# Woven tiles at tiles 11 and 14 of each sixteen, and two explicit orders, in a linear-attention and RWKV feed-forward kernel

## The chip, the cores and the metric

The kernel runs on one core of a Trainium2 chip. A core has a matrix engine (TensorE; PE in the profile, PEld for its weight loads), a vector engine (VectorE; DVE), an activation engine (ScalarE; ACT), GpSimd (POOL) and SyncE (SP), whose queue issues nearly every DMA of this kernel. Each engine takes its own instructions in the order in which the program lists them and waits, where one needs it, on another engine or a DMA. The metric is the device time of one execution in microseconds (us); lower is better.

## The reference, cut to what matters

`x` is (16, 1024, 512) in float32. One post-norm layer is an attention half and a feed-forward half:

```python
qkv = x @ Wqkv.T + bqkv;  q, k, v = split(qkv)
q, k = rope(heads(rmsnorm(q, gq))), rope(heads(rmsnorm(k, gk)))
qf, kf = relu(q), relu(k)
vk  = einsum('bhlp,bhld->bhpd', [v, 1], kf)      # summed over all l of a batch
res = einsum('bhpd,bhld->bhlp', vk, qf)
attn = res[..., :-1] / (res[..., -1:] + EPS_LIN)
x = layernorm(x + rmsnorm(attn @ Wout.T + bout, gout))
# feed-forward: xr, xk mix each row with the row before it
r = sigmoid(xr @ W_r.T);  k = relu(xk @ W_k.T) ** 2
x = layernorm(x + r * (k @ W_v.T))
```

Because `vk` is a sum over a whole batch of 1024 rows, the output of a batch can't begin before all its keys are done.

## The kernel before, in words

The 16 x 1024 rows are cut into 128 tiles of 128 rows, eight to a batch. The program has two stages.

**The key stage** runs over the tiles i = 0 to 127, `early(i)` for the first eight and `slot(i)` for the rest. A plain slot has 36 matmuls of 128x512 on TensorE: 24 for q and k (`proj`, L429), and 12 that add the tile's keys to the batch's sum (`add_kx`, L505, of tile i-1). The projections don't start from zero: a ScalarE copy first puts the bias into the PSUM bank (`seed`, L163; the tiles `psq` and `psk`). On VectorE a slot has the rotary products (`rope`, L461 to L463), the small `ss` (L470), `kl` (L476, the low half of the keys), and the low halves `xl` (L334) and `xnl` (L349) of the next tile's input. q goes out to DRAM (`q_d`, L466).

**Pairs.** When two batches are done, their sums are turned into the combined matrix `m` (value projection, mask, output weights) over the ten slots with i % 16 from 2 to 11: `split_kx` (L588, L589), `finish_pair` (L606, L614, L623 to L635), and `finish_c` (L691 to L695), which multiplies by the output weights with three matmuls into `psm`, splits the result on ScalarE and VectorE into `m`, and stores it. At i % 16 = 1 `finish_a` and `finish_s` empty the sums of a batch out of PSUM and reduce them. `split_kx` and its followers are VectorE's and ScalarE's extra load in these slots.

**Woven tiles.** The output of attention for tile j needs `m` of its batch. For the first eight tiles j = 0 to 7 it is done inside the key stage, woven into its slots, and for j = 8, 9 and 10 a part of it. With FIRST = 30 and STEP = 8 a woven tile j begins at slot i = 30 + 8j: that slot issues the loads of q and x (L209, L225) on SP's queue; the next has `part_q` (L234 to L241: the VectorE instruction `pr`, which is the first to need the loaded q, then a reduction, three small ones, and the scaling of q) and `part_qt` (four transposes on TensorE into `psqt`, L169, then `qth` on ScalarE and `qtl` on VectorE, L252 and L253); the one after has `part_s` (the bias seeded into `psy`), `part_m` (12 matmuls into `psy`, L184) and `part_y` (norm, residual, layer norm: L298 to L306 and L281 to L289). So a woven tile has 16 matmuls of its own on TensorE. The even j begin at i % 16 = 14, the odd ones (38, 54, 70, 86, 102) at i % 16 = 6, in the middle of a pair's ten slots. `load_ks` and `load_m` bring what the woven tiles of a batch read: `ksb` (read by `pr`) and four `mb` (read by `part_m`); both are buffers that batch 1 takes over from batch 0. `late_load` and `late_split` (L720, L722) bring in and split the weights of later stages at slots with i % 16 over 10, through the `xw` buffers, which the loaded x of tiles j >= 4 use too.

Four PSUM banks serve all of `psq`, `psk`, `psqt`, `psy`, `pskv` and `psm` in turn.

**The feed-forward stage** then does the remaining tiles, 128 of feed-forward and 119 of attention output, at some 1450 us.

**What sets the order.** The list of each engine is made at compile time by a planner: it walks the program with estimated durations, and at each point gives an engine the earliest traced instruction that it estimates to be ready. So an instruction that is traced later can be put ahead of one traced earlier. `not_before(ins, last)` (L95) puts an edge into the plan, without a semaphore: `ins` comes after `last` in its engine's list. `in_order` does so for a whole block, and `tc.issue_after(load.ins)` for DMA issues: they come behind the load of `xt` of the same slot.

Of the kernel before, what the change touches and what calls it, by code (L numbers as in the profile page):

```python
# [8 lines left out]
F32 = mybir.dt.float32  # L9
# [6 lines left out]
P = 128  # L16
DIM = 512
# [3 lines left out]
HH = DH // 2  # L21
NPRE = 8
NQ = 3
FIRST, STEP = 30, 8
PAIRS = 7
NWARM = 8
HT = 512
NT = HT // P
# [6 lines left out]
def kernel(  # L35
# [28 lines left out]
    nc = tc.nc  # L64
# [6 lines left out]
    dram = ctx.enter_context(tc.tile_pool(name="dram", bufs=1, space=bass.MemoryType.DRAM))  # L71
# [23 lines left out]
    def not_before(ins, last):  # L95

        tc.add_manual_dep(
            ins,
            last.name,
            mybir.DependencyInfo(mybir.DependencyClass.NoSync, mybir.DependencyReason.DATA),  # L100
            reason="in_order",
        )

    def last_of(engine):
        return next(i for i in reversed(nc.cur_bb.bb.instructions) if i.engine == engine)
# [18 lines left out]
    def bank(name, k=None):  # L124
        if k is not None:
            banks[0] = k
        k = banks[0] % 8
        banks[0] += 1
        if "ps" in own and k >= 4:
            return own["ps"].tile([P, DIM], F32, tag="mm2", bufs=4, name=name)  # L130
        return pp.tile([P, DIM], F32, tag="mm", bufs=4, name=name)
# [69 lines left out]
    def load_ks(b):  # L201
        ksb[b] = ring("ks", b + (b > 0), 1, 1, [P, DIM], F32, f"ksb{b}")
        nc.sync.dma_start(
            out=ksb[b], in_=ks_d[b].rearrange("g p -> (g p)").partition_broadcast(P)
        )

    def load_q(j):
        qs[j] = tp.tile([P, DIM], F32, tag="q", bufs=3, name=f"q{j}")
        nc.sync.dma_start(out=qs[j], in_=q_d[j])  # L209
# [10 lines left out]
    def load_x(j, src=None, early=False):  # L220
        if early and j >= NT:
            xs[j] = tp.tile([P, DIM], F32, tag="xw", bufs=3, name=f"xw{j}")
        else:
            xs[j] = x_tile(j)
        nc.sync.dma_start(out=xs[j], in_=x[j] if src is None else src)  # L225
# [4 lines left out]
    def part_q(j):  # L230

        q = qs[j]
        pr = tp.tile([P, DIM], F32, tag="y", bufs=2, name=f"pr{j}")
        V.scalar_tensor_tensor(pr, q, 0.0, ksb[j // 8], ALU.max, ALU.mult)  # L234
        den = small(HEADS, "den", f"den{j}")
        V.reduce_sum(den, heads(pr), AX.X)
        rs = rstd_all[:, j, 0:1]
        V.tensor_scalar(den, den, rs, EPS_LIN, ALU.mult, ALU.add)
        V.reciprocal(den, den)
        V.tensor_scalar(den, den, rs, None, ALU.mult)  # L240
        V.scalar_tensor_tensor(  # L241
            heads(q), heads(q), 0.0, den.unsqueeze(2).to_broadcast([P, HEADS, DH]), ALU.max, ALU.mult
        )

    def part_qt(j):
        q = qs.pop(j)
        ps = bank(f"psqt{j}")
        transposes(ps, [q[:, c * P : (c + 1) * P] for c in range(NC_)])
        ps = groups(ps)
        th = wp.tile([P, NC_, P], F32R, tag="qth", bufs=2, name=f"qth{j}")  # L250
        tl = wp.tile([P, NC_, P], F32R, tag="qtl", bufs=2, name=f"qtl{j}")
        S.copy(th, ps)  # L252
        V.tensor_sub(tl, ps, f32(th))  # L253
        qT[j] = th, tl
# [3 lines left out]
    def part_s(j):  # L258
        seeds[j] = seeded(f"psy{j}", b_out)

    def part_m(j):
        th, tl = qT.pop(j)
        ps = seeds.pop(j)
        m = [ms[j // 8, c] for c in range(NC_)]
        product(
            ps,
            [((th[:, c, :], tl[:, c, :]), (m[c][:, 0, :], m[c][:, 1, :])) for c in range(NC_)],
            slice(0, P),
            every,
            afresh=False,  # L270
        )
        return ps
# [18 lines left out]
    def part_y(j, ps):  # L291
        for _ in part_y_steps(j, ps):
            pass
# [17 lines left out]
    with ExitStack() as a_ctx:  # L311
# [372 lines left out]
        def finish_c(b, g, place=None):  # L684

            th, tl = fin.pop((b, g))
            if g == 0:
                m_d[b] = dram.tile([P, 2, NC_, DIM], F32, name=f"m_d{b}")
            ps = bank(f"psm{b}{g}", place)
            for n, (a, r) in enumerate(((th, 0), (th, 1), (tl, 0))):  # L690
                T.matmul(ps, lhsT=a, rhs=w_o[g][:, r, :], start=(n == 0), stop=(n == 2))  # L691
            m = te.tile([P, 2, DIM], F32R, tag="m", bufs=2, name=f"m{b}{g}")
            S.copy(m[:, 0, :], ps)
            V.tensor_sub(m[:, 1, :], ps, f32(m[:, 0, :]))
            nc.sync.dma_start(out=m_d[b][:, :, g, :], in_=f32(m))  # L695
# [190 lines left out]
        def late_step(i, load):  # L886
            if staged and staged[0][0] <= i - 2:
                late_split()
            if i == 7:
                with tc.issue_after(load.ins):  # L890
                    constants()
            if i == 12:
                for n in "kr":
                    V.tensor_scalar(omm[n], mu[n], -1.0, 1.0, ALU.mult, ALU.add)

            if late and (3 <= i < 11 or i % 16 > 10 and not 27 <= i < 32):
                with tc.issue_after(load.ins):
                    late_load(i)


        loads_m = {28 + c: (0, c) for c in range(NC_)}
        loads_m.update({n: (1, c) for c, n in enumerate((95, 96, 97, 103))})

        def slot(i):
            last = i == N - 1
            if i + 2 < N:
                load = load_xt(i + 2)
            b, t = divmod(i - 2, 8)
            if b >= 0 and t == 7:
                finish_a(b)  # L910
            qk = [ahead.pop((i, j)) if (i, j) in ahead else proj(i, j) for j in range(2)]
            if not last:
                split_x(i + 1)
            split_xn(i)
            if not last:
                load_xn(i + 1)
            if b >= 0 and t == 7:
                finish_s(b)

            p, u = divmod(i - 18, 16)  # L920
            if 0 <= p < PAIRS and u in (0, 2, 4, 6):
                split_kx(p, u // 2)
            if 0 <= p < PAIRS and u in (1, 3, 5, 7):
                finish_pair(p, u // 2)
            if 0 <= p < PAIRS and 2 <= u < 10:
                finish_c(2 * p + u % 2, u // 2 - 1)
            if i == 8 * 2 * PAIRS + 10:
                finish_b(2 * PAIRS)
            if 0 <= i - 8 * 2 * PAIRS - 11 < NC_:
                finish_c(2 * PAIRS, i - 8 * 2 * PAIRS - 11)  # L930
            add_kx(i - 1)
            for j in range(2):
                rope(i, j, qk[j])
            add_keys(i)
            if not last:
                for j in range(2):
                    rope_table(i + 1, j)
                for j in range(2):
                    seed(i + 1, j)
            if i + 2 < N:  # L940
                late_step(i, load)
            if 0 <= p < PAIRS and u in (0, 1, 3, 4, 5, 7):
                with tc.issue_after(load.ins):
                    if u % 4 == 0:
                        load_ksv(p, u // 4)
                    else:
                        load_wo(u // 2)
            u = i - 8 * 2 * PAIRS - 9
            if 0 <= u < NC_:
                with tc.issue_after(load.ins):  # L950
                    (load_wo, load_wo_last)[u % 2]((0, 2, 1, 3)[u])
            j, late_by = divmod(i - FIRST, STEP)
            if i in loads_m:
                with tc.issue_after(load.ins):
                    load_m(*loads_m[i])
            if j + 1 in (0, NPRE) and late_by == STEP - 1:
                with tc.issue_after(load.ins):
                    load_ks((j + 1) // 8)
            if 0 <= j < NPRE + NQ:
                b = j // 8  # L960
                if late_by == 0:
                    with tc.issue_after(load.ins):
                        load_q(j)
                        load_x(j, early=j < NPRE)
                if late_by == 1:
                    part_q(j)
                    if j <= NPRE:
                        part_qt(j)
                if late_by == 2 and j < NPRE:
                    part_s(j)  # L970
                    part_y(j, part_m(j))
                    if j >= NT:
                        x1_d[j] = dram.tile([P, DIM], F32, name=f"x1_d{j}")
                        nc.sync.dma_start(out=x1_d[j], in_=xs.pop(j))

        x1_d = {}
        tp.tile([P, 56], F32, name="fill_top")
# [299 lines left out]
```

## Time and profile before

| What | us |
|---|---|
| three runs | 2741.31, 2741.24, 2738.0 (median 2741.24) |
| the profiled execution, its own time | 2739.19 |
| its span, first to last instruction | 2737.4 |
| TensorE busy in the span | 2689.9 (98%) |
| VectorE, ScalarE, GpSimd busy | 2197.7, 1909.8, 696.0 |
| mean granted TensorE clock | 0.997 |

The span is from the first to the last instruction that the profiler saw. An engine's busy time leaves out its waits; TensorE's busy time is a union of matmuls whose ends are modelled and overlap, so a stretch that is all busy need not be at full rate. A stretch is best read by three numbers together: its length, the number of matmuls in it, and the clock granted.

In the span the key stage takes about the first 1225 us and the feed-forward stage the rest. In what follows "tile 37 begins at 337.0" means the start of the first `psq` matmul of that tile (L429) in the trace.

### The profile page before, as it was taken

The page shows a single profiled execution, that of the slowest core. Times are in us where ns is not written, and L with a number is a line of the kernel's source. Part 1 is how long each engine was busy: PE and PEld are TensorE (multiplying, and loading weights), DVE is VectorE, ACT ScalarE, POOL GpSimd, SP SyncE. Part 2 cuts the span into 40 slices and gives each one's busy share as a digit, 9 for nine tenths or more (in the row PEclk, how much of TensorE's full clock was granted, in tenths as well). Part 3 has the DMA queues.
Part 4 walks back from the last instruction along what each step waited for, and adds up shares of the span by engine and source line. Part 5 has one row for each costly group of instructions (what it writes and reads, how often), then busy time and mean ns, then how long its engine had stood idle before and what let it go on. Part 6 is the DMA issues. An engine that isn't in the chain of part 4 may idle for free.

```text
span 2737.4 us, 39858 instructions
## 1 busy us (share of the span) xinstructions
PE 2689.9 (98%) x12336; PEld 2214.0 (81%) x12336; DVE 2197.7 (80%) x4852; ACT 1909.8 (70%) x3876; POOL 696.0 (25%) x800
## 2 busy tenths in 40 slices
PE   9999999999999999999999999999999999999998
PEld 7888877777787878887888888888888888888887
DVE  8787777878787887876888888888887888888874
ACT  6666666656666666656778777777777777777775
POOL 5222212222221222224322222222222222222221
PEclk9999999999999999999999999999999999999999
DMA  7888777877777887874323231323223232313210
GB/s 258 291 291 285 235 244 261 270 246 246 234 229 241 265 283 242 277 270 155 108 73 97 94 115 58 113 88 104 74 93 112 63 107 89 119 56 106 79 52 37
DMA packets 241005, 455.80 MB, mean 167 GB/s; under 512 B 25476, under 2 KB 29316, under 8 KB 240792
## 3 DMA queue, kind: packets, MB, share of 16 engines
q1 hardware_dynamic: 240500, 452.73, 51.0%
q8 instruction: 97, 1.59, 0.2%
q14 instruction: 116, 0.95, 0.1%
q10 hardware_dynamic: 292, 0.53, 0.1%
HBM read 334.64 MB, written 118.52 MB: 166 GB/s over the span
## 4 chain that ended last, share of the span: by engine, by line
PE 61%; DVE 3%; DMA 1%; ACT 1%; issue 1%; POOL 0%; POOLq 0%; SPq 0%; DVEq 0%; ACTq 0%
PE psr L184 13%; PE psk L184 12%; PE psv L184 12%; PE psy L184 12%; PE psk L429 3%; PE pskx L505 3%; PE psq L429 3%; PE pst L169 2%; PE psqt L169 2%; PE psm L691 1%; DMA xn<-in_x_dram 0%; DVE t L461 0%; DMA xt<-in_xt_dram 0%; DVE ro L463 0%; DMA q<-q_d 0%
## 5 line engine op out<-in xcount | busy, mean ns | idle before, releaser
L184 PE MATMUL psk<-mkh,w_k 128*128 128x512 f32 x1024 | 332.7, 396 | 1.0 <-DVE kx L531 0.7
L184 PE MATMUL psv<-w_v,kah 128*128 128x512 f32 x1024 | 321.6, 395 | 0.5 <-DVE qtl L253 0.3
L184 PE MATMUL psy<-mb,qth 128*128 128x512 f32 x1024 | 320.2, 390 | 0.4 <-ACT qth L252 0.2
L184 PE MATMUL psr<-w_r,mrh 128*128 128x512 f32 x1024 | 318.6, 396 | 0.0
L184 PEld LDWEIGHTS psy<-mb,qth 128*128 128x128 f32 x1024 | 191.9, 188 | 41.0 <-ACT psy L163 0.8
L487 POOL TENSOR_TENSOR acc<-acc,ro 128x512 f32<-128x512 f32 x96 | 152.7, 1591 | 282.5 <-ACT ro L475 183.3
L184 PEld LDWEIGHTS psk<-mkh,w_k 128*128 128x128 f32 x1024 | 191.2, 188 | 40.1 <-DVE kx L531 0.9
L148 POOL TENSOR_TENSOR rstd_all<-ss,mhalf 128x2 f32<-128x2 f32 x128 | 91.7, 716 | 501.6 <-DVE ss L470 391.5
L184 PEld LDWEIGHTS psr<-w_r,mrh 128*128 128x128 f32 x1024 | 188.7, 188 | 36.8 <-ACT r L1065 0.2
L184 PEld LDWEIGHTS psv<-w_v,kah 128*128 128x128 f32 x1024 | 187.6, 188 | 37.8 <-DVE gate L1155 0.7
L429 PE MATMUL psq<-wqk_h,xh 128*128 128x512 f32 x512 | 202.7, 396 | 15.4 <-ACT psq L163 14.5
L1030 POOL TENSOR_TENSOR mkl<-mixk,mkh 128x512 fp32r<-128x512 f32 x127 | 165.8, 1306 | 181.7 <-ACT mkh L1028 181.7
L429 PE MATMUL psk<-wqk_h,xh 128*128 128x512 f32 x512 | 200.7, 393 | 3.8 <-ACT psk L163 3.8
L429 PE MATMUL psq<-wqk_h,xl 128*128 128x512 f32 x512 | 200.2, 392 | 0.0
L184 PE MATMUL psv<-w_v,kal 128*128 128x512 f32 x512 | 200.1, 391 | 0.0
L429 PE MATMUL psk<-wqk_l,xh 128*128 128x512 f32 x512 | 200.1, 392 | 0.0
L184 PE MATMUL psk<-mkl,w_k 128*128 128x512 f32 x512 | 199.8, 391 | 0.2 <-DVE mkl L1030 0.2
L429 PE MATMUL psq<-wqk_l,xh 128*128 128x512 f32 x512 | 200.0, 392 | 0.0
L429 PE MATMUL psk<-wqk_h,xl 128*128 128x512 f32 x512 | 199.9, 391 | 0.0
L184 PE MATMUL psy<-mb,qtl 128*128 128x512 f32 x512 | 199.6, 390 | 0.0
L184 PE MATMUL psr<-w_r,mrl 128*128 128x512 f32 x512 | 196.5, 393 | 0.0
L474 ACT ACTIVATE kh<-ro,rstd_all 128x512 fp32r<-128x512 f32 x128 | 92.9, 726 | 115.3 <-DVE ro L463 96.5
(208 smaller groups left out, 7119.0 us busy)
## 6 DMA issues: line engine op xcount, KB each, us to landing
tab<-tab_d SPq DMA_DIRECT2D x480, 256.0 KB, 4.5
xt<-in_xt_dram SPq DMA_DIRECT2D x128, 256.0 KB, 4.3
xn<-in_x_dram SPq DMA_DIRECT2D x128, 256.0 KB, 4.5
q_d<-ro SPq DMA_DIRECT2D x128, 256.0 KB, 4.2
m_d<-m SPq DMA_DIRECT2D x64, 512.0 KB, 5.4
mb<-m_d SPq DMA_DIRECT2D x64, 512.0 KB, 6.4
q<-q_d SPq DMA_DIRECT2D x128, 256.0 KB, 2.6
out_dram<-x SPq DMA_DIRECT2D x128, 256.0 KB, 2.0
```

The costliest lines, as they stand in the source:

```text
L148: G.tensor_tensor(dst, src, mhalf[:, 0 : src.shape[1]], ALU.pow)
L169: T.matmul(ps[:, n * P : (n + 1) * P], lhsT=b, rhs=ident, is_transpose=True, start=(n == 0), stop=(n == NC_ - 1), skip_group_check=True,)
L184: T.matmul(ps, lhsT=a[u][:, rows], rhs=b[w][:, cols], start=(afresh and c == 0 and k == 0), stop=(c == n - 1 and k == 2), skip_group_check ...
L429: T.matmul(ps, lhsT=a[i][:, c, :], rhs=w_qk[b][:, c, cols], start=(not seeds and n == 0), stop=(seeds and n == 3 * NC_ - 1), skip_group_ch ...
L474: S.activation(kh, r, AF.Relu, scale=rstd_all[:, i, 1:2])
L487: G.tensor_add(acc[b], acc[b], ros[i])
L505: T.matmul(ps_kx[b][c], lhsT=a[:, c * P : (c + 1) * P], rhs=r, start=(t == 0 and n == 0), stop=(t == 7 and n == 2),)
L691: T.matmul(ps, lhsT=a, rhs=w_o[g][:, r, :], start=(n == 0), stop=(n == 2))
L1030: (V if by_v else G).tensor_sub(ml, m, f32(mh))
```

## The change

A list `WOVEN` takes the place of FIRST and STEP: woven tile j begins at slot `WOVEN[j]`. The even j keep their slots (30, 46, 62, 78, 94, 110); the odd ones move five slots later, from 38, 54, 70, 86, 102 to 43, 59, 75, 91, 107, which is i % 16 = 11. With them move the loads of q and x, `part_q`, `part_qt`, `part_s`, `part_m`, `part_y` and, for j = 5 and 7, the store of x. `late_load` leaves out the slots in `WOVEN`: before, its loads after slot 15 were at 43, 44, 45, 46, 47, 59 and 60; now at 44, 45, 47, 60, 61, 63 and 76. Two of the loads of `m` of batch 1 go from slots 97 and 103 to 108 and 109. `load_ks` of batch 1 stays at slot 93.

Two explicit orders are added. In the woven tiles, the first VectorE instruction of `part_q` (`pr`) comes, in VectorE's list, after the VectorE instruction traced last before it; that is `kl` of its slot, or the last instruction of a `late_split`. In `finish_c`, the first output-weight product comes, in TensorE's list, after the TensorE instruction traced last before it: the end of `proj`, or of `finish_pair` in the slots that have one.

```diff
-FIRST, STEP = 30, 8
+
+WOVEN = (30, 43, 46, 59, 62, 75, 78, 91, 94, 107, 110)
...
+    def behind(engine):
+
+        return last_of(engine), len(nc.cur_bb.bb.instructions)
+
+    def follow(engine, mark):
+        before, n = mark
+        not_before(next(i for i in nc.cur_bb.bb.instructions[n:] if i.engine == engine), before)
...
             ps = bank(f"psm{b}{g}", place)
+            mark = behind(mybir.EngineType.PE)
             for n, (a, r) in enumerate(((th, 0), (th, 1), (tl, 0))):
                 T.matmul(ps, lhsT=a, rhs=w_o[g][:, r, :], start=(n == 0), stop=(n == 2))
+            follow(mybir.EngineType.PE, mark)
...
-            if late and (3 <= i < 11 or i % 16 > 10 and not 27 <= i < 32):
+            if late and (3 <= i < 11 or i % 16 > 10 and not 27 <= i < 32 and i not in WOVEN):
...
-        loads_m.update({n: (1, c) for c, n in enumerate((95, 96, 97, 103))})
+        loads_m.update({n: (1, c) for c, n in enumerate((95, 96, 108, 109))})
...
-            j, late_by = divmod(i - FIRST, STEP)
...
-            if j + 1 in (0, NPRE) and late_by == STEP - 1:
+            for j in (0, NPRE):
+                if i == WOVEN[j] - 1:
+                    with tc.issue_after(load.ins):
+                        load_ks(j // 8)
+            if i in WOVEN:
+                j = WOVEN.index(i)
                 with tc.issue_after(load.ins):
-                    load_ks((j + 1) // 8)
-            if 0 <= j < NPRE + NQ:
-                b = j // 8
-                if late_by == 0:
-                    with tc.issue_after(load.ins):
-                        load_q(j)
-                        load_x(j, early=j < NPRE)
-                if late_by == 1:
-                    part_q(j)
-                    if j <= NPRE:
-                        part_qt(j)
-                if late_by == 2 and j < NPRE:
-                    part_s(j)
-                    part_y(j, part_m(j))
...
+                    load_q(j)
+                    load_x(j, early=j < NPRE)
+            if i - 1 in WOVEN:
+                j = WOVEN.index(i - 1)
+                mark = behind(mybir.EngineType.DVE)
+                part_q(j)
+                follow(mybir.EngineType.DVE, mark)
+                if j <= NPRE:
+                    part_qt(j)
+            if i - 2 in WOVEN[:NPRE]:
+                j = WOVEN.index(i - 2)
+                part_s(j)
+                part_y(j, part_m(j))
...
```

More of the change, by code (lines that the diff above doesn't have):

```diff
@@ L955, in slot @@
                     load_m(*loads_m[i])
-            if j + 1 in (0, NPRE) and late_by == STEP - 1:
-                with tc.issue_after(load.ins):
-                    load_ks((j + 1) // 8)
-            if 0 <= j < NPRE + NQ:
-                b = j // 8
-                if late_by == 0:
-                    with tc.issue_after(load.ins):
-                        load_q(j)
-                        load_x(j, early=j < NPRE)
-                if late_by == 1:
-                    part_q(j)
-                    if j <= NPRE:
-                        part_qt(j)
-                if late_by == 2 and j < NPRE:
-                    part_s(j)
-                    part_y(j, part_m(j))
-                    if j >= NT:
-                        x1_d[j] = dram.tile([P, DIM], F32, name=f"x1_d{j}")
-                        nc.sync.dma_start(out=x1_d[j], in_=xs.pop(j))
+            for j in (0, NPRE):
[4 more added lines that the diff above has]
+                j = WOVEN.index(i)
+                with tc.issue_after(load.ins):
+                    load_q(j)
[11 more added lines that the diff above has]
+                part_y(j, part_m(j))
+                if j >= NT:
+                    x1_d[j] = dram.tile([P, DIM], F32, name=f"x1_d{j}")
+                    nc.sync.dma_start(out=x1_d[j], in_=xs.pop(j))
         x1_d = {}
```

## The prediction

> **What bounds the kernel now.** I read the engine totals first, then stretches of the span, then the one VectorE instruction that the change pins. TensorE is busy 2689.9 of 2737.4 us, so all that can be won is in the 47.5 us in which it idles and in what those gaps cost beside it. The feed-forward stage has none: from 1350 to 2700 us every 50 us are 50.00 us busy. The losses are in the key stage, so I cut it by tiles. First seven tiles each, i % 16 from 5 to 11, the middle of a pair to its end: tiles 21 to 27, which have no woven tile, then 37, 53, 69, 85 and 101, where an odd woven tile runs.
>
> ```profile
> core 0: us, PE busy (x) PEld busy (x) DVE busy (x) ACT busy (x) POOL busy (x), PEclk, DMA share, GB/s
> 191.10:256.80 65.70, 65.70 (x296) 54.53 (x295) 55.26 (x95) 43.35 (x91) 14.48 (x13) 1.00 0.84 271
> 337.00:416.40 79.40, 74.06 (x317) 59.87 (x316) 62.81 (x116) 48.79 (x103) 15.76 (x16) 0.96 0.76 246
> 498.80:576.00 77.20, 71.97 (x313) 58.24 (x312) 61.77 (x111) 48.58 (x103) 15.15 (x15) 0.98 0.77 245
> 658.30:733.80 75.50, 70.05 (x312) 56.86 (x311) 59.70 (x109) 47.72 (x102) 15.49 (x15) 1.00 0.76 247
> 816.60:894.00 77.40, 71.71 (x313) 57.98 (x312) 60.67 (x111) 47.88 (x101) 15.02 (x15) 0.98 0.76 244
> 972.60:1042.50 69.90, 66.32 (x296) 54.33 (x295) 58.75 (x103) 44.13 (x93) 14.03 (x13) 1.00 0.85 275
> ```
>
> Columns: stretch, its length, TensorE busy and its matmuls, and so on; after the brackets the granted clock. The pair alone (first row) keeps TensorE busy to the last hundredth, though VectorE is already 84% busy (55.26 of 65.70). With a woven tile in it, it does not. Next the six tiles with i % 16 from 14 to 3: first 110 to 115 with no output of a woven tile, then 46, 62 and 78 with an even one.
>
> ```profile
> 1057.00:1110.60 53.60, 53.60 (x240) 44.42 (x239) 44.19 (x76) 33.85 (x74) 12.75 (x12) 1.00 0.75 237
> 430.00:489.20 59.20, 57.05 (x251) 46.01 (x250) 48.20 (x85) 36.58 (x79) 11.53 (x13) 1.00 0.77 256
> 590.50:648.50 58.00, 57.24 (x251) 45.92 (x250) 47.05 (x81) 35.31 (x75) 12.92 (x14) 1.00 0.73 238
> 748.30:806.80 58.50, 57.51 (x252) 45.91 (x252) 46.23 (x80) 35.18 (x77) 13.36 (x14) 1.00 0.71 219
> ```
>
> Then the view of the line of `pr`, and two spots of the order of time: VectorE in tile 37, TensorE some us later.
>
> ```profile
> L234 DVE SCALAR_TENSOR_TENSOR pr<-q,ksb x128: 676/681/1709, 274.5 to 2639.3; 128x512 f32<-128x512 f32 x128
> ...
>   DMA q<-q_d: 25.1, 10
> ```
> ```profile
> 342.07 0.69 DVE L349 TENSOR_TENSOR xnl<-xn,xnh 128x512 fp32r<-128x512 f32 x1 [0.72 <-ACT xnh L348]
> 345.80 0.69 DVE L234 SCALAR_TENSOR_TENSOR pr<-q,ksb 128x512 f32<-128x512 f32 x1 [3.04 <-DMA q<-q_d]
> ```
> ```profile
> 347.86 1.19 PE L505 MATMUL pskx<-kl,xnh 128*128 128x512 f32 x4 [1.37 <-DVE kl L476]
> 350.56 0.79 PE L429 MATMUL psq<-wqk_h,xh 128*128 128x512 f32 x1 [1.50 <-ACT psq L163]
> ```
>
> `pr` stands in VectorE's list before q has landed: VectorE sits 3.04 us, with `kl`, the rotary products and thereby the freeing of the `psq` bank behind it, and then TensorE waits for `kl` and for the bank's new bias. All ten such waits are of woven tiles; together 25.1 us.
>
> **The change part by part.** A matmul of 512 columns takes 0.228 us (12 in 2.73 us), a woven tile's own TensorE work is 12 x 0.228 + 4 x 0.057 (128 columns, a quarter) = 2.96 us, and it moves but does not vanish.
>
> 1. *The odd woven tiles leave the pairs.* Excess of a row over the first: length, less 65.70, less the woven tile's 2.96, less 0.228 for each other matmul more. 79.40 - 65.70 - 2.96 - 5 x 0.228 = 9.6; 77.20: 8.3 (one more); 75.50: 6.8; 77.40: 8.5 (one more); 69.90: 4.2 (this one has only `part_q`, no products of its own). Sum **37.4 us**. I take it as all gone, as the first row shows a pair without a woven tile at no idle time. Tile 101 also divides the cost of the others: some 4.2 us are `part_q` (its `pr` waited 3.74 us for its DMA), the other 4 or so are the output products and the norm, after which `psq` waits 1.9 us for its bias.
>
> 2. *They land in tiles 11 to 13 of the sixteen, two in a row with the even ones.* The trace has no two woven tiles so close. Lower bound 0: the first woven tile, in tiles 28 to 33 (263.2 to 310.3), has TensorE busy 47.10 of 47.10. Upper bound the even ones' excess: 59.20 - 53.60 - 2.96 + 5 x 0.228 (251 is 11 more than 240, and 16 are its own) = 3.8; 58.00: 2.6; 58.50, with four: 2.9. Tiles 94 to 99, with transposes alone, last 55.3: 1.5. VectorE has room, less than it seems: a stretch of tiles 108 to 113 has it busy 38.20 of 49.40 with one `part_q` (2.7 us from 0.68 x 4 and three small ones); with two whole woven tiles at some 6 us each (59.70 and 61.77 less 55.26 are 4.4 and 6.5) in its place it would be 35.5 + 12 of 49.4 + 5.9, 86%. So I take 1.3 for each of the four whole ones, 0.6 for j = 9: **+5.8**, from 0 to 4 x 3.8 + 1.5 = 16.7.
>
> 3. *`pr` behind the VectorE instruction traced before it.* `kl` of its slot runs late: that of tile 47 at 457.8, while `pr` stood at 429.1 and its q was scaled at 436.1, 14 us before the transposes that read it (450.4). So the DMA, 2.6 us from issue to landing, is always in time and VectorE's waits (3.2, 3.4, 2.9 and 2.6 us at the even tiles) go. But the chain from `pr` to the scaled q, 4.4 to 7.4 us with what is mixed in, begins up to 29 us later: twice the slack. Transposes and products fall a slot or two later, into tiles 2 to 4, where the pair begins. What waits behind `pr` on VectorE is what came before it anyway; what waits for it is `psqt` on TensorE, with 36 matmuls a tile that can go first. Gain at most the even tiles' whole excess, 3.8 + 2.6 + 2.9 + 1.5 = 10.8; loss at most the 4.2 us that products in a pair cost beyond `part_q`, four times, less what is there now: 16.8 - 10.8 = +6. I take **+1.5**, near the middle.
>
> 4. *The first output-weight product behind `proj` or `finish_pair`.* In the stretch of tiles 21 to 27 all 21 of these matmuls run without an idle hundredth. The one wait of 1.34 us (`psm` at 511 us, its bank not yet emptied by `m`) is in item 1. Cost **0**; its cover is the 24 matmuls of the next `proj`, and without them it is that 1.3 us, five pairs or 6.5.
>
> 5. *SP's queue.* Five loads of q and x, and two stores of x, go later in it, none more in all; per tile it already has xt, xn, four tables and q's store. Two loads of weights move to 63 and 76; the split of the first falls into tile 65, where ScalarE is busiest (0.6 us there, 0.7 on VectorE). `ksb` of batch 1, still issued at slot 93, must now wait for the `pr` traced in slot 92, and `mb` at 95 for its products at 93: what is queued behind on SP is the next tile's xt and tables. Bounds 0 and twice the longest wait for a DMA here, 2 x 3.7; taken **+0.5**, as these sit at 92 to 96 alone.
>
> Sum: -37.4 + 5.8 + 1.5 + 0 + 0.5 = -29.6. The profiled span goes from 2737.4 to 2707.8. That execution took 2739.19 with what lies around the span; the median of the runs, 2741.24, is 3.84 over the span, and so 2707.8 + 3.84 = **2711.6**, said as 2711.
>
> **A rule that speaks against it.** In the rows above the granted clock is below 1.00 only where TensorE has gaps (0.96, 0.98, 0.98), though the longest gap is 2.0 us; 0.04 x 79.4 + 0.02 x 77.2 + 0.02 x 77.4 = 6.2 us, part of the 37.4. The Trainium skill, "TensorE: Matmul & The Clock Gate", Part 1, has the clock gated after an idle window of about 3.4 us; by it gaps of 2 us gate nothing, the dips have another cause and stay, and the sum would be -23.4, or 2717.8. The row with 1.00 and gaps (658.3) is on its side, all rows without gaps on the other; I go by the rows.
>
> **The rivals.**
> - *The losses move with the woven tiles.* Two in a row plus late weights crowd the four PSUM banks, and item 2 and 3 cost their upper bounds: -37.4 + 16.7 + 6 + 0.5 = -14.2, 2727. For it: the even ones lose 2.6 to 3.8 in light tiles now. Against: a good part of that is the wait of `pr` that goes. 0.18.
> - *The pin makes q late, and TensorE waits at the transposes: slower.* If the planner believes VectorE earlier than the chip is, `psqt` stands in TensorE's list before q is scaled, and the wait is up to the chain's 4.4 to 7.4 us, at all eight transposes of tiles 0 to 7. With the 5.8 of item 2 it decides from (37.4 - 5.8) / 8 = 4.0 us each; at 6 us: -37.4 + 5.8 + 48 = +16, 2757.6. For it: the plan already put `pr` 3 us too early ten times. Against: VectorE lags by one or two us, not by a chain, and the order is planned with the pin in it. 0.12.
> - *It does not do what it says.* The planner pulls the moved parts back, or the pairs lose their time to something else: within 5 us of before, 2741. Against: the rows of tiles 21 and 110. 0.06.
>
> **How the numbers follow.** The forecast has 0.64: 2699 (item 2 at 0, a part of item 3's gain) to 2721 by itself. Down to all losses gone is 2741.24 - 37.4 - 10.8 = 2693; the crowded case ends at 2727, and with a wait on SP at 2732. So 2699 to 2732 leaves out the slower and the idle case and a little below. A measurement of this kernel tells some 0.2%, 5.5 us, from no change. Faster: 0.64 + 0.18 = 0.82; within: 0.06; slower: 0.12.
>
> **What would show it.** Right: stretches of tiles 5 to 11 with some 66 us and no idle time; `pr` without waits for its DMA; clock 1.00 through the key stage. Wrong: TensorE idle before `psqt` or `psy` with q's scaling or `qtl` named; new waits for `psq` or `psk` biases in tiles 12 to 4; `xt` or the tables late at tile 93 to 96.

## The result, and the profile after

| | median us | runs | ratio to before, 95% interval |
|---|---|---|---|
| before | 2741.31 | 5 | |
| after | 2783.26 | 5 | 1.0149 [1.0134, 1.0164] |

The changed kernel is 42 us slower. The profiled execution has a span of 2781.8 us (before 2737.4) and a mean granted clock of 0.989 (before 0.997). The forecast, 2711, was wrong in sign.

First the stretches of tiles 5 to 11 of the sixteen, as they were cut before the change: tiles 21, 37, 53, 69, 85 and 101 begin them. Columns as before: stretch, length, TensorE busy and its matmuls, then the other engines, the granted clock, DMA.

```profile
core 0: us, PE busy (x) PEld busy (x) DVE busy (x) ACT busy (x) POOL busy (x), PEclk, DMA share, GB/s
192.60:258.30 65.70, 65.70 (x296) 54.53 (x295) 56.59 (x97) 44.18 (x93) 14.49 (x13) 1.00 0.87 277
345.90:411.80 65.90, 65.90 (x297) 54.70 (x296) 56.47 (x97) 43.65 (x93) 14.50 (x13) 1.00 0.88 281
511.90:577.60 65.70, 65.70 (x296) 54.53 (x295) 56.07 (x96) 43.80 (x92) 14.46 (x13) 1.00 0.89 283
681.40:747.10 65.70, 65.70 (x297) 54.54 (x296) 54.76 (x93) 43.43 (x91) 14.22 (x13) 1.00 0.87 279
850.30:916.30 66.00, 66.00 (x298) 54.76 (x298) 56.90 (x97) 44.46 (x95) 14.46 (x13) 1.00 0.88 283
1014.40:1080.10 65.70, 65.70 (x297) 54.54 (x296) 55.79 (x96) 43.44 (x92) 14.46 (x13) 1.00 0.88 283
```

All six are now alike and TensorE has no idle time in them: what the woven tiles cost inside the pairs is gone, as forecast. Now the rest of each sixteen, tiles 12 to 3 (the first row: tiles 31 to 35), where the woven tiles are.

```profile
281.00:336.30 55.30, 50.15 (x215) 40.47 (x214) 39.16 (x70) 31.46 (x67) 11.18 (x12) 0.97 0.63 195
411.80:502.20 90.40, 77.31 (x332) 61.61 (x331) 62.69 (x115) 49.90 (x106) 19.68 (x19) 0.96 0.65 212
577.60:672.50 94.90, 82.73 (x335) 66.09 (x335) 65.43 (x121) 51.01 (x106) 19.94 (x20) 0.91 0.67 211
747.10:840.80 93.70, 79.79 (x331) 63.70 (x330) 59.19 (x111) 48.36 (x102) 18.27 (x19) 0.95 0.59 185
916.30:1005.50 89.20, 78.07 (x323) 63.41 (x322) 60.83 (x108) 46.67 (x97) 18.42 (x17) 0.92 0.66 206
```

Here TensorE idles 5 to 14 us a row, some 55 in all, and its mean clock falls to 0.91. VectorE is not the bound: 62.69 of 90.40 is 69%. The view of the groups of TensorE says what ended the idle time (behind the second bar: idle us, and by whom). First three groups before, then the same three after.

```profile
L429 PE MATMUL psq<-wqk_h,xh 128*128 128x512 f32 x512 | 202.7, 396 | 15.4 <-ACT psq L163 14.5 <-ACT wqk_h L762 0.7
...
L505 PE MATMUL pskx<-kh,xnh 128*128 128x512 f32 x512 | 148.5, 394 | 8.4 <-ACT kh L474 6.9 <-ACT tab L392 1.4
...
L169 PE MATMUL psqt<-ident,q 128*128 128x128 f32 x512 | 76.9, 272 | 0.0
```
```profile
L438 PE MATMUL psq<-wqk_h,xh 128*128 128x512 f32 x512 | 205.7, 402 | 20.9 <-ACT psq L172 20.0 <-ACT wqk_h L773 0.9
...
L514 PE MATMUL pskx<-kh,xnh 128*128 128x512 f32 x512 | 154.6, 408 | 29.1 <-ACT kh L483 27.9 <-ACT tab L401 1.2
...
L178 PE MATMUL psqt<-ident,q 128*128 128x128 f32 x512 | 79.0, 277 | 8.9 <-DVE q L250 8.8
```

Waits for `kh` went from 6.9 us to 27.9, for a seed of `psq` from 14.5 to 20.0; a wait of the transposes for the scaled q, which would be the obvious harm of the order, is only 8.8. (The lines moved by 9 to 14: `pr` is L243 now, q's last scaling L250, the seeds L172.) And `pr` has no wait left, 25.1 us before:

```profile
L243 DVE SCALAR_TENSOR_TENSOR pr<-q,ksb x128: 675/681/1799, 295.8 to 2683.6; 128x512 f32<-128x512 f32 x128
its engine sat idle before it (us, times) until:
```

Now tile 45, the slot after `part_q` of j = 1, in order of time; first VectorE, then ScalarE, then TensorE (start, duration, engine, line, what; in brackets the idle time before).

```profile
426.08 0.69 DVE L485 TENSOR_TENSOR kl<-ro,kh 128x512 fp32r<-128x512 f32 x1 [0.69 <-ACT ro L484]
426.69 1.80 DVE L243 SCALAR_TENSOR_TENSOR pr<-q,ksb 128x512 f32<-128x512 f32 x1
...
434.46 0.69 DVE L250 SCALAR_TENSOR_TENSOR q<-q,den 128x512 f32<-128x512 f32 x1
```
```profile
433.78 0.72 ACT L483 ACTIVATE kh<-ro,rstd_all 128x512 fp32r<-128x512 f32 x1 [3.93 <-DVE ro L472]
434.53 0.72 ACT L484 ACTIVATE ro<-ro,rstd_all 128x512 f32<-128x512 f32 x1
435.16 0.58 ACT L172 COPY psq<-b_qk 128x512 f32<-128x512 f32 x1
```
```profile
428.12 1.07 PE L514 MATMUL pskx<-kl,xnh 128*128 128x512 f32 x4
434.55 2.08 PE L514 MATMUL pskx<-kh,xnh 128*128 128x512 f32 x4 [5.36 <-ACT kh L483]
...
438.10 0.60 PE L178 MATMUL psqt<-ident,q 128*128 128x128 f32 x4
438.45 0.48 PE L438 MATMUL psq<-wqk_h,xh 128*128 128x512 f32 x1
```

`pr` does stand right behind `kl`, as ordered, and q is scaled at 434.46. The seed for tile 46's `psq`, which has nothing to do with q, comes at 435.16, behind `kh` of tile 45, although ScalarE sat idle for 3.93 us before `kh`. So TensorE, through with everything of tiles 43 to 45 but the keys of 45, has no projection to go on with: it waits 5.36 us for `kh`, does the keys, the transposes, and only then begins tile 46.

### The profile page after: what moved, and what is told of

It reads as the page before. It is cut to its first block, busy times and chain, and to the rows that moved or that the text cites. A ratio compares the mean times of both kernels' runs of the same rounds, so it can differ in the third digit from the quotient of the medians.

```text
span 2781.8 us, 39825 instructions
## 1 busy us (share of the span) xinstructions
PE 2705.6 (97%) x12336; PEld 2228.5 (80%) x12336; DVE 2202.1 (79%) x4852; ACT 1912.2 (69%) x3876; POOL 700.8 (25%) x800
## 4 chain that ended last, share of the span: by engine, by line
PE 50%; DVE 1%; ACT 0%; issue 0%; POOL 0%; POOLq 0%; ACTq 0%
PE psk L193 12%; PE psv L193 12%; PE psr L193 12%; PE psy L193 11%; PE pst L178 2%; PE psqt L178 2%; ACT x L298 0%; DVE mixr L1028 0%; DVE q L250 0%; DVE mixk L1028 0%; DVE gate L1169 0%; DVE qtl L262 0%; DVE mrl L1044 0%; ACT gate L1157 0%; DVE den L247 0%
## 5 line engine op out<-in xcount | busy, mean ns | idle before, releaser
L514 PE MATMUL pskx<-kh,xnh 128*128 128x512 f32 x512 | 154.6, 408 | 29.1 <-ACT kh L483 27.9
```

The lines of the kernel that those rows point to most:

```text
L514: T.matmul(ps_kx[b][c], lhsT=a[:, c * P : (c + 1) * P], rhs=r, start=(t == 0 and n == 0), stop=(t == 7 and n == 2),)
```

## The experiments

Theory A: the order on q's scaling makes the loss, because q's transposes are traced ahead of the next tile's seeds, and the four PSUM banks go out in traced order; a late q holds up the transposes' bank and with it seeds that don't need q. A2: the order makes the loss because it puts `pr` and its chain late into VectorE's list. B: two woven tiles so close are too much wherever they stand. C: the order on the output-weight products.

Time of all (medians; the ratio is to the kernel before on the same chip). The kernel before itself took 2739.77 to 2746.40 us beside these runs, so a difference of some 5 us between runs that were not taken together can't be told from none.

| run | us | ratio, 95% interval |
|---|---|---|
| no_dve_order | 2707.39 | 0.9862 [0.9842, 0.9882] |
| no_pe_order | 2779.15 | 1.0128 [1.0109, 1.0148] |
| no_orders | 2705.87 | 0.9871 [0.9857, 0.9885] |
| before_dve_order | 2757.94 | 1.0049 [1.0032, 1.0067] |
| turn_later | 2739.73 | 0.9982 [0.9973, 0.9992] |
| turn_two_later | 2758.83 | 1.0059 [1.0044, 1.0075] |
| both_later | 2728.32 | 0.9956 [0.9939, 0.9973] |
| order_earlier | 2720.71 | 0.9921 [0.9908, 0.9933] |
| order_last | 2726.92 | 0.9942 [0.9925, 0.9958] |
| load_earlier | 2702.75 | 0.9857 [0.9844, 0.9871] |
| moved_load_earlier | 2701.17 | 0.9856 [0.9841, 0.9871] |

**Which part of the change.** Four runs take one part out or put one in.

`no_dve_order`:

```diff
-                mark = behind(mybir.EngineType.DVE)
                 part_q(j)
-                follow(mybir.EngineType.DVE, mark)
```

> The changed kernel without the order on q's scaling; places and the order on the output-weight products stay. Theory A (the order alone makes the loss: q is scaled late, so its transposes take their PSUM bank late and the next tile's seeds stand behind them): the seven to eight us lost at each woven tile go, pr waits for its DMA again (some 25 us in all), and the time is what was forecast for the moved tiles, 2700 to 2725 us. Theory B (two woven tiles close together are too much wherever they are put): still over 2765 us. Theory C (the order on the products): no change, 2783.

2707.39 us. The order on q's scaling, one edge in the plan at each of the eleven woven tiles, costs 76 us; B and C fall. TensorE now waits 2.4 us for `kh`, 5.7 us for seeds of `psq` and not for q (27.9, 20.0 and 8.8 us with the order). `pr` waits 17.0 us for its DMA again, not the 25 expected. Its last stretch, tiles 92 to 99 and half of 100, where j = 7 and 8 are, has no idle hundredth and needs 77.00 us:

```profile
861.00:938.00 77.00, 77.00 (x347) 63.80 (x346) 64.01 (x114) 50.26 (x107) 21.82 (x20) 1.00 0.83 269
```

`no_pe_order` leaves out `behind` and `follow` in `finish_c`.

> The changed kernel without the order on the output-weight products. Theory A and B: within 6 us of the changed kernel (2777 to 2789 us), since the pairs lose nothing with it. Theory C: down to 2700 to 2725 us.

2779.15 us, 4 below the changed kernel, as A and B had it.

`no_orders` leaves out both.

> The changed kernel without either order, the moved tiles alone. Theory A: 2702 to 2715 us, the order on the output-weight products being worth at most a few us either way.

2705.87 us; its interval and that of `no_dve_order` overlap. The order on the products is worth nothing that can be told here.

`before_dve_order` puts `behind` and `follow` around `part_q` of the kernel before, at the old places.

> The kernel before with the order on q's scaling alone, woven tiles at their old places. Theory A: pr's 25 us of waits go, and each of the eight full woven tiles costs six to eight us at its transposes instead, so about 2765 to 2800 us. Theory B: the order helps where it is, 2705 to 2735 us.

2757.94 us against 2746.40: slower, so the order does harm at the old places too, but by 12 us and not the 24 to 59 expected. `pr`'s waits of 25 us went there too. Tile 40 in the middle of a pair, with j = 1, is 11.3 us long (9.3 before the order); tiles 32, 80 and 96, with an even j, 18.5, 22.4 and 20.3 (10.4, 11.0 and 9.1). The traces show what goes with it: q is scaled 8.6 to 9.8 us into the tile with its transposes at the odd j, in the pairs, and 9.1 us at tile 48 (j = 2), which is 12.4 us long (9.9 before); at tiles 32, 64, 80 and 96 it is 14.7 to 16.7 us. Why q is less late in the pairs no run tells.

**Late chain or late bank.** In `turn_later` `part_qt(j)` goes from slot i - 1 to slot i - 2 of `WOVEN`, to stand ahead of `part_s(j)`; the order stays.

```diff
             if i - 1 in WOVEN:
...
-                if j <= NPRE:
-                    part_qt(j)
+            if i - 2 == WOVEN[NPRE]:
+                part_qt(NPRE)
             if i - 2 in WOVEN[:NPRE]:
                 j = WOVEN.index(i - 2)
+                part_qt(j)
                 part_s(j)
```

> The changed kernel with q's transposes traced one slot later, after that slot's seeds and before the seed of psy; the order on q's scaling stays as it is. Theory A with PSUM banks given out in traced order: the next tile's seeds no longer stand behind the transposes, the waits of TensorE for kh and for the seed of psq beside each woven tile go, and the time falls to 2690 to 2725 us though pr runs as late as in the changed kernel. Rival A2 (what costs is pr's chain itself, which holds up VectorE's rotary products and thereby kh): no change, 2775 to 2790 us. Theory B: over 2765 us.

2739.73 us: 43 of the 76 us are back, between the two, and out of the range of each. TensorE's waits for `kh` fell from 27.9 to 4.6 us and those for q from 8.8 to none, as A had it; those for seeds of `psq` did not, 22.4 us after 20.0. But at tile 45 the seed came early: in this run tile 45 begins at 414.8, and

```profile
416.08 0.59 ACT L172 COPY psq<-b_qk 128x512 f32<-128x512 f32 x1
```
```profile
431.04 0.69 DVE L250 SCALAR_TENSOR_TENSOR q<-q,den 128x512 f32<-128x512 f32 x1
```

the seed of tile 46 comes 1.2 us into tile 45, while q is scaled 16.2 us in, as late as in the changed kernel. Tile 45 takes 8.2 us, not 20.3. What stayed stands one tile later, `psq` waiting for its seed 3.55 us at tile 48. This edit has both `psqt` and `psy` between two tiles' seeds; with four banks given out in turn, the next `psq` then gets the bank of the `psq` just before it. Two runs were to settle that.

`turn_two_later`: `part_qt`, `part_s`, `part_m` and `part_y` all in slot i - 3, `turn_later` with 3 for 2.

> The changed kernel, order on q's scaling kept, with the transposes and the output products both traced two slots after the scaling instead of none and one. Theory A: what was left after one slot later (2739.73 against 2707.39 us without the order) is the same effect, seeds traced after the transposes that still wait for them; with q scaled a whole slot before its transposes it goes, 2700 to 2722 us. Rival A2 (what is left is pr's chain on VectorE, late and mixed with the rotary products): stays at 2732 to 2745 us.

2758.83 us, a miss of both theories: slower than one slot later. The loss is again where `psqt` and `psy` stand together, and now falls into the pair as well, which takes banks for `pskv` (tiles 35 and 51 take 19.8 and 16.4 us, in `turn_later` 11.6 each).

`both_later`: `part_qt` in slot i - 2, the rest in slot i - 3, so that seeds stand between `psqt` and `psy`.

```diff
+            if i - 2 in WOVEN[: NPRE + 1]:
+                part_qt(WOVEN.index(i - 2))
+            if i - 3 in WOVEN[:NPRE]:
+                j = WOVEN.index(i - 3)
                 part_s(j)
```

> The changed kernel, order on q's scaling kept, transposes traced one slot later and the output products one slot after them, so that psqt and psy no longer take two of the four banks one after the other between two tiles' seeds (as they do when both are traced in one slot). Theory A: what stayed in the two runs with one slot for both (2739.73 and 2758.83 us) came from that pair of banks; 2702 to 2728 us here. Rival A2 (pr's late chain on VectorE costs by itself): 2735 us or more.

2728.32 us, 0.3 above A's range and out of A2's: 55 of the 76 us are back with the order still there. Tiles 45 to 47 take 0.5 us in all beyond their matmuls (10.7 in the changed kernel; a matmul of 512 columns is counted as 0.228 us, a shorter one in proportion); the 21 us left are nearly all beside the even j, whose transposes and products now fall into tiles 49 to 51, where the pair begins (2.44 us for the seed of `psq` there at 452.6). Some 11 of them are at j = 6 and 8, where q is again scaled 12 and 13 us into the tile with its transposes. That the rest is the crowding of the pair is argued and not shown.

**How late is too late.** `order_earlier` orders `pr` behind `kl` of the slot that issues its load, one slot earlier:

```diff
             if i in WOVEN:
                 j = WOVEN.index(i)
+                marks[j] = last_of(mybir.EngineType.DVE)
...
-                mark = behind(mybir.EngineType.DVE)
+                n = len(nc.cur_bb.bb.instructions)
                 part_q(j)
-                follow(mybir.EngineType.DVE, mark)
+                follow(mybir.EngineType.DVE, (marks.pop(j), n))
```

> The changed kernel with q's scaling ordered behind kl of the slot that issues its load, one slot earlier than in the changed kernel; transposes and products as there. Theory A: the order is not bad in itself, it is one slot too late; pr has no wait for its DMA or a short one, the waits for kh and for seeds beside the woven tiles are gone, and the time is that without the order or a little less, 2697 to 2712 us. Rival (any order on pr puts VectorE's list in a shape that costs): over 2740 us.

2720.71 us, 9 over A's range and far under the rival's bound: 13 over the run without the order. Nearly all of that is at tiles 93 and 96 (13.9 and 17.2 us long, against 8.7 and 10.4 without the order); at 96 q is still scaled 14 us into the tile. The waits for `kh` and for seeds of `psq` are down to 6.1 and 8.4 us, not gone.

`order_last` orders the last instruction of the scaling in place of the first:

```diff
-                follow(mybir.EngineType.DVE, mark)
+                not_before(last_of(mybir.EngineType.DVE), mark[0])
```

> The changed kernel with the order on the last VectorE instruction of q's scaling (the product that makes the scaled q) in place of the first, so that pr and the reduction run early again, with their wait for the DMA, and one instruction of 0.7 us alone is late. Theory A (what costs is that the transposes, and with them their bank and the seeds behind it, come late): most of the loss stays, as the scaled q is only some four us earlier than in the changed kernel; 2750 to 2785 us. Rival A2 (the cost is the whole chain from pr put late into VectorE's list): 2705 to 2735 us.

2726.92 us, in A2's range and out of A's. By itself that speaks for A2: with the chain early and one instruction late, three quarters of the loss go. But A's range rested on q being some four us earlier; it was seven (9.2 us into tile 45, not 16.3). One table of tile 45 holds all, in us from its first projection, worked out from starts in the order of time:

```
run              q scaled   seed of psq 46   transposes   tile 45 takes
no_dve_order      -13.9          6.4             5.4           8.7
order_earlier       8.5         10.3            11.2          11.5
order_last          9.2          9.6            11.1          11.5
after              16.3         17.0            19.9          20.3
turn_later         16.2          1.2            18.8           8.2
both_later         15.9          1.2            18.5           8.2
```

Where the transposes are traced ahead of the seed (first four rows), the seed follows the start of q's scaling by 0.4 to 1.8 us if q is later than the seed's own time of some six us, and tile 45 grows with it. Where they are traced behind it (last two), it comes at 1.2 us and the tile has its 8.2 us, with the chain from `pr` as late as ever. So the late q harms by way of the seeds, and A2's chain by itself costs tile 45 nothing. The seed doesn't wait on the chip for q: in `order_last` it starts 0.4 us after q's last instruction starts, which takes 0.69 us. What holds it is its place in ScalarE's list: behind `kh` of tile 45 in `order_earlier`, `order_last` and the changed kernel, ahead of it in the other three rows. Behind `kh`, it also waits out what `kh` waits for on VectorE (3.93 us in the changed kernel), and there the chain, mixed in on VectorE, can count. Controls of the same kind stand in the changed kernel itself: j = 9 has the order and no transposes, and tiles 107 to 110 of it lose nothing; j = 10, likewise without transposes, loses some 2 us at tile 113, where TensorE waits 1.96 us for `kh`; j = 8 has transposes and no products, and tile 96 takes 21.1 us (10.4 without the order). That the planner puts the seed there because it hands out the banks in traced order fits every row but is inferred from these times; no trace shows the banks.

**A version that beats both.** `load_earlier`: without the order on q's scaling, q's load issued one slot earlier.

```diff
+            if i + 1 in WOVEN:
+                with tc.issue_after(load.ins):
+                    load_q(WOVEN.index(i + 1))
             if i in WOVEN:
                 j = WOVEN.index(i)
                 with tc.issue_after(load.ins):
-                    load_q(j)
                     load_x(j, early=j < NPRE)
```

> The changed kernel without the order on q's scaling, and q loaded one slot earlier. The 17.0 us that pr still waits for its DMA in the run without the order should go. If these waits cost TensorE anything at the new places, the time falls below 2707.39 us, to 2698 to 2704; if VectorE has the room for them there, it stays within 3 us of it.

2702.75 us, a gain of 4.6 on `no_dve_order` that the two intervals don't separate. `pr` waited 11.7 us, not none: the plan moved it forward with its load.

`moved_load_earlier` is the same without the order on the products.

> The moved tiles with q loaded one slot earlier and neither order. Theory A, with both orders dispensable: the better of the two runs with one of these edits, 2698 to 2706 us, under both the kernel before and the changed one.

2701.17 us, 1.4% under before. The page of its profile:

```profile
span 2697.7 us, 39845 instructions
## 1 busy us (share of the span) xinstructions
PE 2675.3 (99%) x12336; PEld 2211.7 (82%) x12336; DVE 2191.0 (81%) x4852; ACT 1915.2 (71%) x3876; POOL 703.7 (26%) x800
```

TensorE idles 22.4 us of the span (before 47.5), at a mean clock of 1.000.

## Why the prediction was wrong

- **Item 1, the odd woven tiles leave the pairs, -37.4: right.** The six rows of tiles 5 to 11 are 65.70 to 66.00 us long with no idle time.
- **Item 2, they land two in a row, +5.8: right in kind, dear by some 4 us at most.** With items 1, 2 and 5 alone the sum was 2741.24 - 37.4 + 5.8 + 0.5 = 2710.1; the moved tiles alone took 2705.87, no further off than these runs tell. (Its row from 263.2 us begins with tile 29, not 28.)
- **Item 3, the order on `pr`, +1.5: the step that failed.** It measured 76 us (2783.26 against 2707.39). The half on the DMA held: no wait of `pr` is left. It was also seen that the chain starts "up to 29 us later: twice the slack". What failed is the sentence that cleared it: "what waits for it is `psqt` on TensorE, with 36 matmuls a tile that can go first". Two thirds of these 36, the projections of the next tile, can't go first: they need their seeds, and these came only after the late q, though they don't read it (that the reason is the bank of `psqt`, handed out ahead of theirs, is inferred). My bound of +6 came from rows in which q had been scaled 8.8 to 23.0 us before the tile with its transposes even began, and so held no row of a late q. An edge behind the instruction *traced* last is not an edge behind one that is *done* early: `kl` of slot 44 runs 8 us into tile 45. And "+1.5, near the middle" was a slip: the middle of -10.8 and +6 is -2.4.
- **Item 4, the order on the products, 0: right**, 4.1 and 1.5 us with nothing in them that these runs tell from none.
- **Item 5, SP's queue, +0.5: right within its size.** Without the order on `pr`, tiles 92 to 99 have no idle time.
- **The clock.** I went by the rows and took the dips as the gaps' own; that held. The traces have the dips as steps of 3.41 us at half clock. The kernel before has four ahead of its last 5 us, all in pairs with an odd woven tile, each straight after 3.4 us in which TensorE idled 1.8 to 2.2 us; `no_orders`, with the odd tiles moved, has none. `no_dve_order` has one, after a gap of 2.4 us in tiles 44 to 51. Not every such gap has one: the row at 658.3 has two of 2.0 us and a clock of 1.00. The Trainium skill, "TensorE: Matmul & The Clock Gate", Part 1, has in its table of states the half clock after at least one idle window of some 3.4 us; TensorE idled less before these steps, so here the measurement decides. The sum with the dips kept was farther off for the moved tiles (2710.1 + 6.2 = 2716.3 against 2705.87).
- **The rivals.** The slower one, which got 0.12, was right in sign and in its cause, a pin that makes q late; it put the wait at the transposes and at 6 us each. There it is 8.8 us of the whole; 47.9 us are waits for `kh` and for seeds (8.1 without the order). "Against: VectorE lags by one or two us, not by a chain" stays open, since no trace shows the planner's estimates; but it cleared nothing, as q was scaled 16 us into tile 45 and the seeds of tile 46 came no sooner. The signs of being wrong did name "new waits for `psq` or `psk` biases". The range left this case out by choice, and that choice, with 0.82 on faster, was a fault of its own: the price of a late q had no row in the trace, and I bounded it by rows in which q was early.

## What to carry to other kernels

An order that takes away a wait moves an instruction to where its new predecessor really runs: look that up in the trace, and follow all that is *traced* behind its consumers, above all what draws on the same ring of buffers, before calling the delay hidden. If a load is late, try to issue it earlier before holding back its reader: here the other cost 76 us, and the one took some 5 us off in each of two comparisons, which these runs don't tell from none. Two parts of a change can be right and wrong at once; each alone on the chip takes one run to tell.

## What was not expected of the hardware

The granted clock fell to a mean of 0.91 and 0.92 in stretches whose longest gaps of TensorE were 5.3 and 4.3 us, and to 0.98 where none was over 2.4 us. Cut finer, these dips are steps to half clock, as in two stretches of the kernel before, one with a gap of 1.96 us and the next:

```profile
394.70:398.10 3.40, 1.44 (x7) 0.98 (x6) 3.37 (x8) 3.40 (x10) 0.45 (x1) 1.00 0.16 42
398.10:401.50 3.40, 3.40 (x10) 2.66 (x9) 3.26 (x7) 0.91 (x2) 0.69 (x1) 0.50 0.88 288
```

In the second TensorE counts as busy throughout, but its matmuls start 0.43 us apart, not 0.23. So the share of idle time understates the loss. Leaving out the last 5 us of each span, the changed kernel has 61 us of such steps, with TensorE busy in 52.6 of them; `no_dve_order` has 3.4 us, busy throughout. TensorE idles 76.2 us of the changed kernel's span and 27.2 us of the other's. Those 49.0 us more, and half of the 49.2 us more of busy time at half clock (an estimate of what the clock cost), make 73.6 of the 75.8 us by which the changed kernel's span is longer.
